# Banded attention layer of a two-layer mixer: both rows' scores ahead of the pair, a bias add behind the differences, two late checks in one place

## Chip, cores and metric

The kernel runs on one core of one Trainium2 chip. The metric is device time in microseconds of the one launch, as the median of three runs. All times below are microseconds unless marked ns. A core has TensorE (PE; its weight loads are listed apart as PEld), VectorE (DVE), ScalarE (ACT), GpSimd (POOL) and SyncE (SP, which issues most of the transfers). Each engine works through its own instructions in order and waits on semaphores of the others.

## What is computed

The input x is 128 rows of 256 positions of 256 channels, in float32. Two layers follow one another, each of the form x = x + layer(group norm of x). Layer 0 is a full attention with a bias from a second input z, a mask, and a gate. The change touches layer 1 alone: in each row an attention with 4 heads of 64 channels, in which position i sees only the positions within 16 of it.

```python
def _L1_conv_ref(x, w_in, b_in, w_out, b_out, band):   # band = 16, 4 heads
    qkv = x2 @ w_in.T + b_in
    q, k, v = jnp.split(qkv, 3, axis=-1)               # each cut into 4 heads of 64
    scores = jnp.einsum('bhid,bhjd->bhij', q, k) / jnp.sqrt(D)
    keep = jnp.abs(i - j) <= band
    attn = jax.nn.softmax(jnp.where(keep, scores, -jnp.inf), axis=-1)
    out = jnp.einsum('bhij,bhjd->bhid', attn, v)
    return out @ w_out.T + b_out
...
x = x + _L1_conv_ref(_gn(x), ...)
```

## The kernel before

**Tiling.** Layer 1 works through the 128 rows as 64 pairs of rows; row 0 and row 1 of a pair have 512 positions together. Channels lie on the partitions, in two chunks of 128 (`KC` = 2). The class `Pair1` holds one pair, and its methods each issue one step.

**The steps of a pair.** The constructor loads the pair twice through SP: `xs` in blocks to be transposed, and `xt` as it is, for the residual. `turn` (line 1860) transposes `xs` on DVE. `centre(k)` (line 1865) normalises one chunk on ACT into `xgT`; in the kernel before, the call for the second chunk also adds the output bias to `xt`, as one POOL instruction over 128x1024 elements (line 1870). `differences` (lines 1877 to 1880) makes four sums and differences of `xgT` on POOL, called t1 to t4, tile `dT`. They serve a scheme that forms the 2 by 2 block product of q, k and v by seven products instead of eight: `product(n, i)` issues product i for q (n = 0), k (n = 1) or v (n = 2) on PE (line 1915, for v line 1911) and, for four of the seven, an ACT instruction that takes the result out of PSUM (line 1924, for v 1922). `join(n, i)` (line 1931) adds a second PSUM tile to what ACT took out, on DVE. Products 6, 5, 7 and 4 read t2, t1, t3 and t4. Product 5 starts the second PSUM tile anew, so it waits for `join(n, 2)`, which reads that tile.

`scores(r)` (line 1968) makes the scores of row r on PE, 16 small products into two PSUM tiles; ACT takes the exponential (line 1977, two instructions) into an SBUF tile `e` with three buffers, and POOL multiplies by the band mask (line 1979, two instructions). `apply(r)` (line 1997) makes the weighted sums of v and the sums of the weights, the latter split over two halves of a PSUM tile. `copy_sums` (line 2012) and `copy_odd` (line 2015) bring them to SBUF on ACT. On DVE follow `join_sums` (line 2018, both inputs in SBUF), `join_odd` (line 2021), `invert` (line 2024, a reciprocal) and `weigh` (line 2029, both inputs in SBUF). `out_row` or `out_block` (line 2045) is the last projection on PE, `keep_row` (line 2053) adds the residual `xt` on DVE, and SP writes the result.

**PSUM.** Layer 1 uses eight PSUM tiles of 512 values a partition: four for what `apply` and the output projection write, and four handed out by `mm1(name, side)`, two buffers on side 0 and two on side 1. q's and v's products take side 0, k's take side 1, and both rows' scores take side 1.

**Order.** The order of the work is written out by hand: inside `tc.manual_schedule()` each engine gets its instructions in the order of the calls. A turn of the loop over p mixes three pairs: `was` (its row 1 is applied and put out), `now` (scores, and row 0 applied) and `nxt` (its products); `nn` is centred and differenced, and `n3` transposed. In the kernel before, `now.scores(0)` opens the turn and `now.scores(1)` stands in its middle, ahead of `now.apply(0)`. At the end of the turn come `nn.centre(1)`, `nn.differences()` and `n3.turn()`; the next turn's first DVE steps are `was.join_sums(1)` and `join(0, 2)`, and its first POOL steps the mask products.

**Checks.** The kernel checks some tiles against bounds on DVE, three instructions each (lines 958 to 960). `guard` checks the reciprocals of the last eight pairs, 128x512 at a time, in the middle of the turn. The others wait in the list `checks` and are taken one a turn: in turns 1 to 55 in the middle behind `guard`, in later ones at the end, behind `n3.turn()`. Four checks of the earlier pairs' sums, loaded in turn 58, fall into turns 58 to 61.

**Ahead of the loop**, pair 0 is centred and projected in full (`project`, line 1939; `values`, line 1954), then pair 1 is centred and differenced; then the mask and layer 0's sums are loaded through SP.

Of the kernel before, what the change touches and what calls it, by code (L numbers as in the profile page):

```python
# [9 lines left out]
F32 = mybir.dt.float32  # L10
# [11 lines left out]
def bcast(ap, axis, n):  # L22

    ap = ap.unsqueeze(axis)
    shape = list(ap.shape)
    shape[axis] = n
    return ap.broadcast_to(shape)
# [746 lines left out]
def fast_kernel(  # L774
# [1006 lines left out]
    with tc.tile_pool(name="l1", bufs=2) as sb, tc.tile_pool(  # L1781
# [5 lines left out]
        def mm1(name, side=0):  # L1787
            return ps_s.tile([P, 512], F32, name=name, tag=f"s{side}")
# [47 lines left out]
        class Pair1:  # L1836
# [25 lines left out]
            def centre(self, k):  # L1862
                if k == 0:
                    self.xgT = sb.tile([P, KC, N2], F32, name="xgT1", tag="xgT")
                nc.scalar.activation(
                    self.xgT[:, k, :], self.xT[:, k, :] if self.p else self.xT[k], AF.Identity,
                    bias=nM1[:, k : k + 1], scale=R1c[:, k : k + 1],
                )
                if k == KC - 1:
                    nc.gpsimd.tensor_tensor(self.xt, self.xt, bcast(bout_r, 1, 2 * NB), ALU.add)  # L1870

            def differences(self):

# [59 lines left out]
            def project(self, which, m):  # L1933
                n = ("qT", "kT").index(which)
                if m == 0:
                    setattr(self, which, sb.tile([P, KC, N2], F32, name=f"{which}1", tag=which))
                ps = mm1("ps_p1")
                for k in range(KC):
                    nc.tensor.matmul(
                        ps, w_in[:, k, n * C + m * P : n * C + (m + 1) * P], self.xgT[:, k, :],  # L1940
                        start=(k == 0), stop=(k == KC - 1),
                    )
                nc.scalar.activation(
                    getattr(self, which)[:, m, :], ps, AF.Identity, bias=bin_c[:, n * KC + m : n * KC + m + 1]
                )

            def values(self, r):
                if r == 0:
                    self.v = sb.tile([P, 2, NB, C], F32, name="v1", tag="v")
                ps = mm1("ps_v1")  # L1950
                for b in range(NB):
                    t = r * NB + b
                    for k in range(KC):
                        nc.tensor.matmul(
                            ps[:, b * C : (b + 1) * C], self.xgT[:, k, t * P : (t + 1) * P], w_in[:, k, 2 * C : 3 * C],
                            start=(k == 0), stop=(k == KC - 1),
                        )
                nc.scalar.copy(self.v[:, r, :, :].rearrange("p b c -> p (b c)"), ps)

            def scores(self, r):  # L1960

                ps = [mm1("ps_sc1", 1) for _ in range(2)]
                at = lambda q, c, j: ps[q][:, (c * 2 + j) * W : (c * 2 + j + 1) * W]
                for c in range(KC):
                    for k in range(NK):
                        for q in range(2):
                            rs = slice(q * D1, (q + 1) * D1)
                            nc.tensor.matmul(  # L1968
                                at(q, c, k // 2)[half(k)],
                                self.kT[rs, c, r * I + k * KB : r * I + (k + 1) * KB],  # L1970
                                self.qT[rs, c, r * I + q0(k) : r * I + q0(k) + W],
                                start=True, stop=True,
                            )
                e = sm.tile([P, 2, KC, NK // 2 * W], F32, name="e1", tag="e", bufs=3)
                ev = e.rearrange("p q c w -> p q (c w)")
                for q in range(2):
                    nc.scalar.activation(ev[:, q], ps[q][:, : KC * NK // 2 * W], AF.Exp)  # L1977
                for q in range(2):
                    nc.gpsimd.tensor_tensor(  # L1979
                        e[:, q], e[:, q], bcast(bw.rearrange("p b w -> p (b w)"), 1, KC), ALU.mult  # L1980
                    )
                self.es[r] = e
# [87 lines left out]
        def check_all(src, lo, hi):  # L2070
            for i in range(0, src.shape[1], 256):
                n = min(256, src.shape[1] - i)
                checks.append(lambda i=i, n=n: check(src[:, i : i + n], lo, hi, sm))

        def load_sums(src, name):
            t = sb.tile([P, src.shape[0] // P], F32, name=name, tag=name, bufs=1)
            nc.sync.dma_start(t, src.rearrange("(a b) -> a b", a=P))
            check_all(t, 1e-16, 1e8)

        with tc.manual_schedule():  # L2080
            now, nxt = pair1(0), pair1(1)
            now.turn()
            norm1()
            mix_weights()
            for k in range(KC):
                now.centre(k)
            nxt.turn()
            for m in range(KC):
                now.project("qT", m)
                now.project("kT", m)  # L2090
            for r in range(2):
                now.values(r)
            for k in range(KC):
                nxt.centre(k)
            nxt.differences()
        check_all(eb.rearrange("p h b i -> p (h b i)"), math.exp(-20.0), math.exp(20.0))
        mask_t = sb.tile([S, I], F32, name="mask_all", bufs=1)
        nc.sync.dma_start(mask_t, mask)
        check_all(mask_t, 1e-15, 1e15)
        load_sums(rsum.rearrange("n q r c i -> (n q r c i)"), "sums0")  # L2100

        with tc.manual_schedule():
            was = Nobody()
            for p in range(NP - 1):
                nn = pair1(p + 2) if p == 0 else n3
                n3 = pair1(p + 3)
                if p == 0:
                    nn.turn()
                if p == NP - LATE + 2:
                    load_sums(rsum1[: NP - LATE].rearrange("n q r i -> (n q r i)"), "sums1")  # L2110

                now.scores(0)
                was.apply(1)
                nxt.begin_fast()
                was.copy_sums(1)
                nxt.product(0, 1)
                was.copy_odd(1)
                nxt.product(1, 1)
                was.join_sums(1)
                for n in range(2):  # L2120
                    nxt.product(n, 2)
                    nxt.join(n, 2)
                was.invert(1)
                for i in (6, 5, 7):
                    for n in range(2):
                        nxt.product(n, i)
                for n in range(2):
                    nxt.join(n, 5)
                was.join_odd(1)
                was.weigh(1)  # L2130
                was.out_row(0)
                for n in range(2):
                    nxt.product(n, 4)
                    nxt.product(n, 3)
                    nxt.join(n, 3)
                fast = p < NP - 2
                if fast:
                    nxt.product(2, 1)
                    nxt.product(2, 2)
                    nxt.join(2, 2)  # L2140
                nn.centre(0)
                was.guard(1)
                if checks and 0 < p < NP - LATE:
                    checks.pop(0)()

                now.scores(1)
                now.apply(0)
                now.copy_sums(0)
                if fast:
                    nxt.product(2, 6)  # L2150
                    nxt.product(2, 5)
                now.copy_odd(0)
                now.join_sums(0)
                was.out_block(1, 0)
                if fast:
                    nxt.product(2, 7)
                now.join_odd(0)
                was.out_block(1, 1)
                if fast:
                    nxt.join(2, 5)  # L2160
                was.keep_row(1)
                if fast:
                    nxt.product(2, 4)
                    nxt.product(2, 3)
                    nxt.join(2, 3)
                now.invert(0)
                now.weigh(0)
                nn.centre(1)
                nn.differences()
                n3.turn()  # L2170
                if checks and p >= NP - LATE:
                    checks.pop(0)()
                was, now, nxt = now, nxt, nn
            assert not checks

# [8 lines left out]
            was.weigh(1)  # L2184
            was.out_row(0)
            now.scores(1)
            now.values(1)
            was.out_row(1)
            was.guard(1)
            now.apply(0)  # L2190
# [90 lines left out]
```

## Time and profile before

| what | us |
|---|---|
| median of 3 runs (lowest and highest) | 3168.44 (3167.47 to 3168.5) |
| the profiled execution's own time | 3168.98 |
| its span, first to last instruction | 3167.0 |
| mean granted TensorE clock | 0.984 |
| PE busy | 3030.7 (96%) |
| DVE busy | 2421.0 (76%) |
| POOL busy | 2292.6 (72%) |
| ACT busy | 1605.8 (51%) |

The profile is one execution. Its page lists busy time by engine, then the chain of work that ended last, then the costliest groups of instructions. Beside the page the trace answers finer questions: a timeline lists instructions by start, with their duration, their count where equal ones are merged, and in brackets the idle time of the engine ahead of them and what ended it; the waits sum up who waited for whom; a table of stretches gives each engine's busy time and the clock granted to PE. A DVE or POOL row's duration includes time in which the instruction has begun and does not get on. Layer 1 fills the time from about 1996 on, some 1165 of the 3167.

### The profile page before, as it was taken

The page shows a single profiled execution, that of the slowest core. Times are in us where ns is not written, and L with a number is a line of the kernel's source. Part 1 is how long each engine was busy: PE and PEld are TensorE (multiplying, and loading weights), DVE is VectorE, ACT ScalarE, POOL GpSimd, SP SyncE. Part 2 cuts the span into 40 slices and gives each one's busy share as a digit, 9 for nine tenths or more (in the row PEclk, how much of TensorE's full clock was granted, in tenths as well). Part 3 has the DMA queues.
Part 4 walks back from the last instruction along what each step waited for, and adds up shares of the span by engine and source line. Part 5 has one row for each costly group of instructions (what it writes and reads, how often), then busy time and mean ns, then how long its engine had stood idle before and what let it go on. Part 6 is the DMA issues. An engine that isn't in the chain of part 4 may idle for free.

```text
span 3167.0 us, 84747 instructions
## 1 busy us (share of the span) xinstructions
PE 3030.7 (96%) x35678; PEld 2112.9 (67%) x35678; DVE 2421.0 (76%) x3983; ACT 1605.8 (51%) x2637; POOL 2292.6 (72%) x1632
## 2 busy tenths in 40 slices
PE   5679999999999999999999999799999999999997
PEld 3345555556555555556555555688888888888886
DVE  7976677777777777777777777588888777777787
ACT  3454444444444444444444444455555555555553
POOL 3459899889888899988988896455555555555553
PEclk9789999999999999999999999899999999999999
DMA  9952333333333333343233432534343434343441
GB/s 360 391 169 52 98 69 97 98 80 82 94 91 70 98 97 95 71 98 92 66 96 92 98 72 65 123 86 98 82 103 82 100 86 97 88 94 91 93 98 36
DMA packets 690966, 328.42 MB, mean 104 GB/s; under 512 B 538672, under 2 KB 639920, under 8 KB 689424
## 3 DMA queue, kind: packets, MB, share of 16 engines
q1 hardware_dynamic: 686176, 320.28, 39.8%
q8 instruction: 282, 4.62, 0.6%
q10 hardware_dynamic: 4400, 2.63, 0.3%
q14 instruction: 108, 0.88, 0.1%
HBM read 254.09 MB, written 68.75 MB: 102 GB/s over the span
## 4 chain that ended last, share of the span: by engine, by line
PE 80%; DVE 9%; issue 5%; DMA 4%; POOL 2%; ACT 0%; SPq 0%; DVEq 0%; POOLq 0%; ACTq 0%
PE ps_p L1357 21%; PE ps_sc L1394 8%; PE ps_qk L1915 8%; PE ps_ov L1429 7%; PE ps_su_y L2045 7%; PE ps_y L1484 7%; PE ps_v L1375 7%; PE ps_qk L1911 7%; DVE rv L2024 3%; PE ps_su L1437 3%; PE ps_o L1997 2%; PE ps_sc L1968 2%; DVE xT L1860 2%; DMA xa<-in_x_dram 2%; DMA zt<-in_z_dram 1%
## 5 line engine op out<-in xcount | busy, mean ns | idle before, releaser
L1418 POOL TENSOR_TENSOR eboth<-e 128x512 f32<-128x512 f32 x512 | 745.6, 1477 | 175.9 <-PE ps_su L1437 95.9
L1414 DVE TENSOR_TENSOR e<-ps_sc,eb 128x1024 f32<-128x1024 f32 x384 | 458.3, 1221 | 288.6 <-ACT ps_sc L1406 288.5
L1979 POOL TENSOR_TENSOR e<-e,bw 128x384 f32<-128x384 f32 x256 | 262.0, 1045 | 487.8 <-ACT e L1977 487.8
L1406 ACT ACTIVATE ps_sc<-ps_sc 128x1024 f32<-128x1024 f32 x384 | 375.4, 1007 | 436.2 <-PE ps_sc L1394 309.7
L1394 PE MATMUL ps_sc<-qT,kT 32*128 32x256 f32 x4096 | 294.1, 400 | 0.8 <-DVE e L1414 0.8
L1394 PEld LDWEIGHTS ps_sc<-qT,kT 32*128 32x128 f32 x4096 | 185.3, 184 | 103.0 <-issue 90.7
L1484 PEld LDWEIGHTS ps_y<-wo,oT 128*128 128x128 f32 x1024 | 194.8, 191 | 84.2 <-issue 44.5
L2045 PE MATMUL ps_su_y<-w_out,oT 128*128 128x256 f32 x1008 | 249.3, 380 | 0.7 <-ACT sums L2012 0.7
L1357 PE MATMUL ps_p<-xnT,wq 128*128 128x512 f32 x512 | 247.6, 606 | 0.8 <-POOL xnT L1344 0.8
L1429 PE MATMUL ps_ov<-e,v 128*32 128x256 f32 x4096 | 248.0, 383 | 0.0
L1357 PE MATMUL ps_p<-xgT,wg 128*128 128x512 f32 x512 | 247.2, 605 | 0.1
L1484 PE MATMUL ps_y<-wo,oT 128*128 128x256 f32 x1024 | 243.5, 381 | 3.5 <-POOL oT L1474 2.7
L1375 PE MATMUL ps_v<-wv,xnT 128*128 128x256 f32 x1024 | 242.0, 379 | 1.6 <-ACT xgT L1326 1.6
L1357 PE MATMUL ps_p<-xnT,wk 128*128 128x512 f32 x512 | 240.6, 592 | 0.0
L1924 ACT ACTIVATE u<-ps_qk,bin_c 128x256 f32<-128x256 f32 x378 | 174.9, 477 | 115.9 <-PE ps_qk L1915 115.7
L1375 PEld LDWEIGHTS ps_v<-wv,xnT 128*128 128x128 f32 x1024 | 194.5, 190 | 55.9 <-issue 31.1
L2024 DVE RECIPROCAL rv<-sums 128x256 f32<-128x256 f32 x128 | 222.7, 1740 | 0.0
L1915 PE MATMUL ps_qk<-dT,wst 128*128 128x256 f32 x756 | 192.4, 391 | 19.0 <-DVE qT L1931 16.1
L2045 PEld LDWEIGHTS ps_su_y<-w_out,oT 128*128 128x128 f32 x1008 | 182.8, 191 | 21.0 <-ACT sums L2012 0.9
L1429 PEld LDWEIGHTS ps_ov<-e,v 128*32 128x32 f32 x4096 | 120.1, 110 | 109.0 <-issue 42.3
L2018 DVE TENSOR_TENSOR sums<-sums 128x256 f32<-128x256 f32 x128 | 104.8, 819 | 107.6 <-ACT sums L2012 107.6
L1915 PEld LDWEIGHTS ps_qk<-dT,wst 128*128 128x128 f32 x756 | 136.9, 191 | 63.8 <-DVE qT L1931 40.7
(229 smaller groups left out, 6470.9 us busy)
## 6 DMA issues: line engine op xcount, KB each, us to landing
xa<-in_x_dram SPq DMA_DIRECT2D x8, 4096.0 KB
xt<-in_x_dram SPq DMA_DIRECT2D x64, 512.0 KB
x<-xo SPq DMA_DIRECT2D x16, 2048.0 KB
xt<-x SPq DMA_DIRECT2D x64, 512.0 KB
rvb<-rsum SPq DMA_DIRECT2D x252, 128.0 KB
xs<-x SPq DMA_DIRECT2D x252, 128.0 KB
out_dram<-yo SPq DMA_DIRECT2D x63, 512.0 KB
xs<-in_x_dram SPq DMA_DIRECT2D x248, 128.0 KB
```

What stands on the lines that cost most here:

```text
L1357: nc.tensor.matmul(ps, w[:, k, m * P : (m + 1) * P], getattr(self, src)[:, k, :], start=(k == 0), stop=(k == KC - 1),)
L1375: nc.tensor.matmul(self.ps_v[:, b * C : (b + 1) * C], self.xnT[:, k, t * P : (t + 1) * P], wv[:, k, :], start=(k == 0), stop=(k == KC - 1),)
L1394: nc.tensor.matmul(self.pss[q // 2][:, q % 2, b, :], self.kT[rs, c, r * I + b * P : r * I + (b + 1) * P], self.qT[rs, c, r * I : (r + 1) * I],
L1406: nc.scalar.activation(self.pss[a], ps, AF.Exp)
L1414: nc.vector.tensor_tensor(es[a], pss[a], eb[:, h : h + 2], ALU.mult)
L1418: nc.gpsimd.tensor_tensor(t, es[a][:, :, 0, :], es[a][:, :, 1, :], ALU.add)
L1429: nc.tensor.matmul(ov[q * D0 : (q + 1) * D0, c, :], self.v[:, r, b, h * D0 : (h + 1) * D0], es[q // 2][:, q % 2, b, :], start=(b == 0), st ...
L1484: nc.tensor.matmul(self.ps_y[:, b * C : (b + 1) * C], self.oT[r][:, k, b * P : (b + 1) * P], wo[:, k, :], start=(k == 0), stop=(k == KC - 1),)
L1915: nc.tensor.matmul(to, lhs, rhs, start=start, stop=True, skip_group_check=True)
L1979: nc.gpsimd.tensor_tensor(e[:, q], e[:, q], bcast(bw.rearrange("p b w -> p (b w)"), 1, KC), ALU.mult)
L2024: nc.vector.reciprocal(self.rv[:, r, :], self.sums[:, 0])
L2045: nc.tensor.matmul(self.y[:, b], self.oT[r][:, k, b * P : (b + 1) * P], w_out[:, k, :], start=(k == 0), stop=(k == KC - 1),)
```

## The change

The diff does five things. `now.scores(1)` goes from the middle of the turn to directly behind `now.scores(0)`, and row r's scores take PSUM side 1 − r, so row 1's are on side 0. The bias add on POOL leaves `centre` and becomes `add_bias`, called for `nn` behind `nn.differences()`, and for pairs 0 and 1 behind pair 0's `values`. Pair 1 is centred in the loop of pair 0's projections, and its differences stand ahead of pair 0's `values`. All turns from 1 on take their check in the middle, behind `guard`. Mask and layer 0's sums are loaded at the start of turn 1, behind the loads of pair 4. `project` takes side m, and the last pair's `values(1)` takes side 1.

```diff
             def centre(self, k):
...
-                if k == KC - 1:
-                    nc.gpsimd.tensor_tensor(self.xt, self.xt, bcast(bout_r, 1, 2 * NB), ALU.add)
+
+            def add_bias(self):
+                nc.gpsimd.tensor_tensor(self.xt, self.xt, bcast(bout_r, 1, 2 * NB), ALU.add)
...
-                ps = mm1("ps_p1")
+                ps = mm1("ps_p1", m)
...
-            def values(self, r):
+            def values(self, r, side=0):
...
-                ps = mm1("ps_v1")
+                ps = mm1("ps_v1", side)
...
-                ps = [mm1("ps_sc1", 1) for _ in range(2)]
+                ps = [mm1("ps_sc1", 1 - r) for _ in range(2)]
...
             for m in range(KC):
                 now.project("qT", m)
                 now.project("kT", m)
+                nxt.centre(m)
+            nxt.differences()
             for r in range(2):
                 now.values(r)
-            for k in range(KC):
-                nxt.centre(k)
-            nxt.differences()
-        check_all(eb.rearrange("p h b i -> p (h b i)"), math.exp(-20.0), math.exp(20.0))
-        mask_t = sb.tile([S, I], F32, name="mask_all", bufs=1)
-        nc.sync.dma_start(mask_t, mask)
-        check_all(mask_t, 1e-15, 1e15)
-        load_sums(rsum.rearrange("n q r c i -> (n q r c i)"), "sums0")
-
-        with tc.manual_schedule():
+            now.add_bias()
+            nxt.add_bias()
+            check_all(eb.rearrange("p h b i -> p (h b i)"), math.exp(-20.0), math.exp(20.0))
+
             was = Nobody()
             for p in range(NP - 1):
...
+                if p == 1:
+                    mask_t = sb.tile([S, I], F32, name="mask_all", bufs=1)
+                    nc.sync.dma_start(mask_t, mask)
+                    check_all(mask_t, 1e-15, 1e15)
+                    load_sums(rsum.rearrange("n q r c i -> (n q r c i)"), "sums0")
...
                 now.scores(0)
+                now.scores(1)
                 was.apply(1)
...
                 was.guard(1)
-                if checks and 0 < p < NP - LATE:
+                if checks and p > 0:
                     checks.pop(0)()

-                now.scores(1)
                 now.apply(0)
...
                 nn.centre(1)
                 nn.differences()
+                nn.add_bias()
                 n3.turn()
-                if checks and p >= NP - LATE:
-                    checks.pop(0)()
                 was, now, nxt = now, nxt, nn
...
-            now.values(1)
+            now.values(1, 1)
```

## The prediction

> **What bounds the kernel now.** I read the page's chain of work first, then a timeline of one pair in the middle of layer 1, then the waits of PE.
>
> ```profile
> PE 80%; DVE 9%; issue 5%; DMA 4%; POOL 2%; ACT 0%; SPq 0%; DVEq 0%; POOLq 0%; ACTq 0%
> ```
>
> The chain is PE's, so a layer-1 pair costs what PE works plus what PE waits. In the timeline every pair has the same shape; this is the start of pair 14 (columns: start, duration, engine, line, operands, count, idle before it).
>
> ```profile
> 2259.80 0.89 PE L1968 MATMUL ps_sc<-qT,kT 64*64 64x96 f32 x32
> 2260.62 0.93 PE L1997 MATMUL ps_o<-e,v 64*32 64x96 f32 x60
> 2262.02 0.69 DVE L2029 TENSOR_TENSOR oT<-odd,rv 128x512 f32<-128x512 f32 x1
> 2262.07 1.24 POOL L1880 TENSOR_TENSOR dT<-xgT,dT 128x256 f32<-128x256 f32 x1
> 2262.63 1.24 DVE L1860 STREAM_TRANSPOSE xT<-xs 128x1024 f32<-128x1024 f32 x1
> 2263.27 2.14 POOL L1979 TENSOR_TENSOR e<-e,bw 128x384 f32<-128x384 f32 x2
> 2263.74 1.03 PE L1915 MATMUL ps_qk<-dT,wst 128*128 128x256 f32 x4
> 2263.79 0.76 DVE L2018 TENSOR_TENSOR sums<-sums 128x256 f32<-128x256 f32 x1
> 2264.47 0.41 DVE L1931 TENSOR_TENSOR qT<-ps_qk,u 128x256 f32<-128x256 f32 x1
> 2264.94 1.99 PE L1915 MATMUL ps_qk<-dT,wst 128*128 128x256 f32 x8 [0.17 <-DVE qT L1931]
> 2271.21 0.89 PE L1968 MATMUL ps_sc<-qT,kT 64*64 64x96 f32 x32
> 2272.03 0.93 PE L1997 MATMUL ps_o<-e,v 64*32 64x96 f32 x60
> 2277.50 0.89 PE L1968 MATMUL ps_sc<-qT,kT 64*64 64x96 f32 x32
> ```
>
> Call S the start of row 0's scores (2259.80). The next pair's S is 2277.50: one pair takes 17.70. Each scores block costs PE 0.82 (2259.80 to 2260.62; 2271.21 to 2272.03). PE has one wait: product 5 of q (the x8 row at 2264.94) overwrites a PSUM tile that DVE's join (2264.47) must have read. That join stands in DVE's queue behind reciprocal, weigh (2262.02), transpose (2262.63) and join_sums (2263.79). The four records before it start at 2263.74; at 0.213 apiece (eight take 1.70) product 5 could start at 2264.59. It starts at 2264.94 and, with its weight load uncovered, works as if from 2265.07 (the following group starts 1.83 later instead of 1.70). The stall is thus **0.48** a pair; PE's own work is 17.22.
>
> Now the point on which the forecast stands: why join_sums takes 0.76. It has two SBUF inputs, and POOL is at work. Rows of other places show what that does:
>
> ```profile
> 254.46 2.34 POOL L1282 TENSOR_TENSOR xt<-xt,bo_r 128x1024 f32<-128x1024 f32 x1
> 255.75 2.13 DVE L1414 TENSOR_TENSOR e<-e,eb 128x1024 f32<-128x1024 f32 x1
> ...
> 2326.84 1.00 POOL L1979 TENSOR_TENSOR e<-e,bw 128x384 f32<-128x384 f32 x1
> 2327.22 0.90 DVE L2018 TENSOR_TENSOR sums<-sums 128x256 f32<-128x256 f32 x1 [1.19 <-ACT sums L2012]
> 2327.80 2.54 POOL L1870 TENSOR_TENSOR xt<-xt,bout_r 128x1024 f32<-128x1024 f32 x1
> ```
>
> The mask multiply ends at 2327.84 and join_sums at 2328.12, 0.28 later, although it began 0.62 before that end. In layer 0 the bias add on POOL ends at 256.80 and DVE's product of two SBUF tiles, begun before, ends 1.08 later, at 257.88; begun with POOL idle such a product takes 1.22. So a two-SBUF DVE instruction that meets a running POOL instruction stands until that one ends. In reverse, dT's fourth difference takes 1.24 behind weigh, 0.73 elsewhere.
>
> The Trainium skill, "SBUF — State Buffer", section "Who interferes with whom", says the same against this change: a DVE instruction with two SBUF inputs contends with a GpSimd one that reads SBUF, and whoever issues first keeps the port for the whole instruction. If the port were shared by turns instead, the stall worked out below would go and the sum would be that of rival A.
>
> **Scores of row 1 beside row 0's, on PSUM side 0.** No instruction is added. PE's 0.82 moves from the middle (2271.21) to S+0.82. Apply of the old row 1 goes from S+0.82 to S+1.64, products 6 to 4.76 (before 3.94), and product 5 could start at 5.61. Side 0 is free in time: its last reader is DVE's join of v, S+0.11 to 0.53. ACT's second pair of exponentials (0.88) ends at 2.76 and product 1, which now takes side 0 after them, starts at 2.97; ACT's copy of the sums starts at 3.14, after apply, so they delay nothing. The three buffers of e suffice: the one taken was read a pair ago. If DVE stayed as it is, product 5 would find its tile at 5.27, before 5.61, and the 0.48 would be gone. What is late next is the bias add.
>
> **The bias add (line 1870) moves from before the four differences to behind them.** POOL's order becomes masks of both rows, differences, bias add. The differences wait as now for ACT's second centre (difference 2 at S+0.89), the fourth ends at S+3.51, and where the mask multiply stands now (2263.27) the bias add starts. It takes 2.34 when DVE leaves it alone (line 1870: least 2.345, median 2.542) and ends at S+5.81 (2265.61). join_sums cannot go ahead of it: DVE is free only at S+3.99. Its end becomes 2265.61 + 0.28 = 2265.89 instead of 2264.55, **1.34 later**, and the join and product 5 behind it likewise: product 5 at S+6.61 instead of 5.27. Both masks follow by S+9.9; row 0's is needed at S+12.7, so that costs nothing. In the middle POOL is now idle under join_sums (0.41 instead of 0.90), but DVE waits there anyway.
>
> After product 5 nothing else changes but the 0.82 that left the middle (the change of tile shape, 0.14, which a scores block pays after the v products, I let apply pay): 12.43 becomes 11.61. The pair takes 6.61 + 11.61 = 18.22, **+0.52**. Bounds: with the bias add at 2.54, +0.72; with the 0.14 not paid, +0.38; with no block at all, −0.48.
>
> **Late checks in one place.** Now a check of the sums, behind the transpose, costs a whole pair 1.79 (three pairs of 19.49) because it feeds the stall; after the last one PE also runs slowly:
>
> ```profile
> 3063.50:3083.00 19.50, 17.70 (x329) 15.23 (x329) 16.98 (x27) 10.41 (x22) 9.73 (x9) 1.00 0.36 82
> 3102.40:3106.00 3.60, 3.52 (x10) 2.85 (x11) 2.48 (x5) 0.95 (x2) 0.00 (x0) 0.64 0.00 0
> ```
>
> (Second column on: length, busy PE, PEld, DVE, ACT, POOL; then granted clock.) Beside the guard (0.41 + 0.69 + 0.69) the check (0.28 + 0.42 + 0.42 without POOL) makes the DVE work of the middle 1.1 longer than it is; the slack there is about 0.5 to the join before product 3 of v, and the first difference of dT can block the guard for up to 0.6. I take a stall of 0.8 (between 0 and 1.2) in pairs 58 to 61: 19.0 each. Now they take 17.70 + 3 × 19.49, and 1.9 for the slow stretch: 78.1 against 76.1, **−2.0**.
>
> The slow stretch came after PE had idled 1.96. The Trainium skill, "TensorE: Matmul & The Clock Gate", section "Part 1: The HAM clock gate", wants an idle window of some 3.4 us before the clock falls; the row shows a clock of 0.64 after less, so here the measurement decides. The new stall leaves PE idle about 1.0, and idling 1.53 in the pair at 3063.50 kept 1.00, so I add nothing.
>
> **Pair 1's input among pair 0's projections; mask and sums loaded later.**
>
> ```profile
> 2011.98 1.99 PE L1915 MATMUL ps_qk<-xgT,w_in 128*128 128x256 f32 x8 [1.67 <-ACT xgT L1865]
> 2016.73 4.33 PE L1915 MATMUL ps_qk<-dT,wst 128*128 128x256 f32 x12 [2.75 <-POOL dT L1878]
> 2024.72 0.93 PE L1997 MATMUL ps_o<-e,v 64*32 64x96 f32 x60
> ```
>
> PE waits 1.67 and 2.75 and runs slowly behind (12 records in 4.13 instead of 2.56). With centre under the projections (ACT idles 1.0 and more between them) and the differences done near 2010.6, PE makes both scores from 2009.42, starts products when the second exponential has left side 0 (near 2011.8), and works 1.83 + 2.56 + 1.73 + 0.99 with some 0.3 of waits: apply at 2019.2 instead of 2024.72, **−5.5** (bounds 0 and −7). The two bias adds and row 0's mask end near 2017.3, in time. Mask and sums loads (0.51 and 0.43 of SP's issue time) pass from ahead of pair 2's input to behind pair 4's, needed three pairs later: nothing; without that cover 0.94 once. The projections' own PSUM sides, and those of the last pair, free no wait that a row shows: nothing. Pair 62 has no v products: its lost scores block (1.2 there) against 0.47 more wait, −0.7.
>
> **Sum**, on the profiled execution (3168.98; span 3167.0 and 1.98 around it; the median of three is 0.54 lower): pairs 1 to 57, 57 × 0.52 = +29.6; late pairs −2.0; pair 62 −0.7; start −5.5. Together +21.4: **3190**.
>
> **Rivals.** A, faster: the block isn't met. It decides at the end of join_sums, 0.53 ahead of product 5: by S+5.1 there would be no stall, by S+5.6 no loss. For it speaks that today's stall is just this queue; against it the rows above, and 0.5 between the bias add's start (3.47) and join_sums (3.99). Pairs at 17.22: 57 × −0.48 = −27.4, late pairs −6.0, pair 62 −1.7, start −5.5: −40.6, **3128**.
> B, slower still: the bias add takes its median of 2.54 and the new neighbours cost 0.14 more at a change of shape: +0.34 × 62 = 21 on top, **3211**. For it: every add of the loop shows about 2.54; against: there DVE's sum was ahead of it in the port.
> C, the change cancels itself: the block lasts, but exponentials or the join of v come too late for side 0, or start and end give more; PE has about 1.0 of slack before product 5, so this hides: 3162 to 3175.
>
> **Numbers.** Forecast 0.68 (3175 to 3203), A and parts of it 0.17 (3125 to 3162), B 0.10 (3203 and more), C 0.05. A measurement here tells 0.2%, 6.3 us, from no change: faster 0.17, same 0.06, slower 0.77. The range 3165 to 3211 leaves out A and the top of B.
>
> **What would show it.** Right: the pair's period at 18.2; join_sums of row 1 lasting 2.1 and ending 0.28 behind the bias add; PE's wait for q's join near 1.0 in each pair; the middle join_sums at 0.41; apply of pair 0 near 10 us behind the first scores. Wrong: join_sums short with the bias add running over it, the bias add behind join_sums, or a period near 17.2.

## The result and the profile after

The changed kernel takes **3187.9** (median of 4 runs, 3187.05 to 3189.77) against 3167.95 (3166.9 to 3168.5) of the kernel before beside it: a ratio of 1.0064, interval 1.0047 to 1.0082. The prediction was 3190, slower. The profiled execution took 3188.32; its span is 3186.6, against 3167.0.

The chain that ended last, on the page of the kernel after, doesn't name the loss: DVE has less of it than before (4% against 9%), PE more.

```profile
PE 87%; issue 4%; DVE 4%; DMA 3%; POOL 2%; ACT 1%; ACTq 0%; SPq 0%; DVEq 0%; POOLq 0%
```

The same chain in order of time shows why, in the pair taken apart below (start, duration, engine or "issue", tile, line, count):

```profile
2318.74 1.94 PE ps_qk L1916 x8
2320.73 1.16 issue
2321.89 0.42 DVE qT L1932
2322.36 1.99 PE ps_qk L1916 x8
```

By the chain the join of q follows PE's work of 2320.7, but starts 1.16 later. Nothing that the chain knows releases it then, so the time is put down to "issue". What DVE did in it, the timeline of the kernel after tells, from row 0's scores on (S = 2315.86; columns: start, duration, engine, line, operands, count, idle before):

```profile
2315.86 1.55 PE L1969 MATMUL ps_sc<-qT,kT 64*64 64x96 f32 x64
2317.34 0.93 PE L1998 MATMUL ps_o<-e,v 64*32 64x96 f32 x60
2318.09 0.69 DVE L2030 TENSOR_TENSOR oT<-odd,rv 128x512 f32<-128x512 f32 x1
...
2319.33 2.35 POOL L1871 TENSOR_TENSOR xt<-xt,bout_r 128x1024 f32<-128x1024 f32 x1
2319.86 2.11 DVE L2019 TENSOR_TENSOR sums<-sums 128x256 f32<-128x256 f32 x1
2321.65 4.05 POOL L1980 TENSOR_TENSOR e<-e,bw 128x384 f32<-128x384 f32 x4
2321.89 0.41 DVE L1932 TENSOR_TENSOR qT<-ps_qk,u 128x256 f32<-128x256 f32 x1
2322.36 1.99 PE L1916 MATMUL ps_qk<-dT,wst 128*128 128x256 f32 x8 [0.69 <-DVE qT L1932]
```

The bias add ends at 2321.68, S+5.82. join_sums, begun 0.53 behind its start, is done at 2321.97, 0.29 behind its end: 2.11 for what took 0.76 before. Then come the join and product 5, for which PE stands idle. From another stretch of the same kernel: two applies of row 1 one pair apart, 18.24, and join_sums of row 0, which no POOL instruction meets in the middle (0.90 before).

```profile
2292.15 0.93 PE L1998 MATMUL ps_o<-e,v 64*32 64x96 f32 x60
...
2310.39 0.93 PE L1998 MATMUL ps_o<-e,v 64*32 64x96 f32 x60
...
2312.59 0.42 DVE L2019 TENSOR_TENSOR sums<-sums 128x256 f32<-128x256 f32 x1
```

The two largest waits of the weight loads in the kernel after from 2040 to 3050 (total, times, longest). The first line is the 1.1 a pair of product 5; not all of its records are in the trace. The second waits for nothing that the profile shows; the kernel before has no such line.

```profile
PEld ps_qk L1916 <- DVE qT L1932: 56.6, 51, 1.2
PEld ps_su_y L1998 <- issue: 8.7, 10, 1.7
```

**Where the time went**, counted from the start of one `join_odd` of row 0, in the middle of a turn, to the next (line 2021 before, 2022 after):

| stretch | before | after | difference | predicted |
|---|---|---|---|---|
| to the first middle | 2027.67 | 2021.62 | −6.05 | −5.5 |
| next 56 pairs | 990.99 | 1022.59 | +31.60 | +29.1 (56 × 0.52) |
| last 7 intervals and tail | 148.31 | 142.38 | −5.93 | −2.2 (0.5 − 2.0 − 0.7) |
| span | 3167.0 | 3186.6 | +19.6 | +21.4 |

### The profile page after: what moved, and what is told of

It is laid out like the page before. It is cut to its first block, busy times and chain, and to the rows that moved or that the text cites. A ratio compares the mean times of both kernels' runs of the same rounds, so it can differ in the third digit from the quotient of the medians.

```text
span 3186.6 us, 84747 instructions
## 1 busy us (share of the span) xinstructions
PE 3021.2 (95%) x35678; PEld 2111.3 (66%) x35678; DVE 2480.1 (78%) x3983; ACT 1600.8 (50%) x2637; POOL 2281.2 (72%) x1632
## 4 chain that ended last, share of the span: by engine, by line
PE 87%; issue 4%; DVE 4%; DMA 3%; POOL 2%; ACT 1%; ACTq 0%; SPq 0%; DVEq 0%; POOLq 0%
PE ps_p L1357 21%; PE ps_qk L1916 11%; PE ps_sc L1394 8%; PE ps_ov L1429 7%; PE ps_su_y L2046 7%; PE ps_y L1484 7%; PE ps_v L1375 7%; PE ps_qk L1912 6%; PE ps_o L1998 3%; PE ps_su L1437 3%; PE ps_sc L1969 3%; PE ps_su_y L1998 2%; DMA xa<-in_x_dram 2%; DMA zt<-in_z_dram 1%; DVE st L1192 1%
## 5 line engine op out<-in xcount | busy, mean ns | idle before, releaser
L1879 POOL TENSOR_TENSOR dT<-xgT,dT 128x256 f32<-128x256 f32 x63 | 46.1, 731 | 300.1 <-ACT xgT L1865 300.1
L1878 POOL TENSOR_TENSOR dT<-xgT 128x256 f32<-128x256 f32 x63 | 45.9, 729 | 236.9 <-ACT xgT L1865 236.9
L2019 DVE TENSOR_TENSOR sums<-sums 128x256 f32<-128x256 f32 x128 | 151.8, 1186 | 53.3 <-ACT sums L2013 53.2
```

## The experiments

The theory T (theory P in the expectations): the loss is join_sums of row 1, a DVE instruction with two SBUF inputs, standing until the whole bias add on POOL ends. Its rivals: Q, the loss comes from the scores' new place and PSUM side; R, the join of q is late for its place in DVE's queue however short join_sums is. The ratios are to the kernel before, run beside each kernel on the same chip; a pair is the median of the 56 intervals counted above.

| kernel | median (runs) | ratio, interval | pair (median) | join_sums row 1 |
|---|---|---|---|---|
| after | 3187.9 (4) | 1.0064, 1.0047 to 1.0082 | 18.23 | 2.11 |
| bias add before the differences | 3151.4 (4) | 0.9948, 0.9931 to 0.9965 | 17.49 | 0.75 |
| late bias add alone | 3260.43 (4) | 1.0293, 1.0276 to 1.031 | 19.05 | 2.10 |
| scores side by side alone | 3160.92 (10) | 0.9979, 0.9969 to 0.9989 | 17.49 | 0.75 |
| late checks alone | 3165.28 (11) | 0.999, 0.9981 to 0.9999 | 17.70 | 0.75 |
| new start alone | 3164.38 (11) | 0.9985, 0.9976 to 0.9994 | 17.70 | 0.75 |
| bias add in four | 3141.43 (4) | 0.9918, 0.9901 to 0.9935 | 17.17 | 0.48 |
| sum from PSUM | 3140.27 (4) | 0.9914, 0.9899 to 0.9929 | 17.31 | 0.38 |
| four adds in POOL's gap | 3141.29 (4) | 0.991, 0.9893 to 0.9926 | 17.17 | 0.75 |
| gap and PSUM | 3141.73 (4) | 0.9916, 0.99 to 0.9933 | 17.17 | 0.38 |
| scores apart, PSUM | 3137.17 (4) | 0.9905, 0.9889 to 0.9922 | 17.33 | 0.38 |
| before, PSUM | 3145.69 (4) | 0.9932, 0.9916 to 0.9949 | 17.33 | 0.39 |

**One line back: the bias add before the differences.**

```diff
 (kernel after)
-                nn.differences()
-                nn.add_bias()
+                nn.add_bias()
+                nn.differences()
```

> The changed kernel with one step put back: in the loop POOL makes the bias add ahead of the four differences again, right behind the four mask products. Theory P (a two-input DVE instruction stands until the running POOL instruction ends): join_sums of row 1 now meets a mask product of 1.0 and ends near S+4.75 instead of S+6.1, so product 5 no longer waits; but the bias add now runs from about S+7.5 to S+9.9, and weigh of row 1, due at about S+8.9, has two SBUF inputs too: it is held up by some 0.9, and through the join behind it product 2 of v waits about 0.5. A pair of about 17.6 instead of 18.24, in all about 3148 (if weigh is not held up, 17.1 and 3117). Rival Q (the cost is the scores' new place: the second pair of exponentials ahead of the sums, and products waiting for side 0): nothing changes, 3188.

In this kernel's timeline join_sums is short and weigh is the one that stands: the bias add ends at 2315.57, weigh 0.55 later. (0.69 is weigh's length with POOL idle.)

```profile
2309.73 0.75 DVE L2019 TENSOR_TENSOR sums<-sums 128x256 f32<-128x256 f32 x1
...
2313.21 2.36 POOL L1871 TENSOR_TENSOR xt<-xt,bout_r 128x1024 f32<-128x1024 f32 x1
...
2314.67 1.45 DVE L2030 TENSOR_TENSOR oT<-odd,rv 128x512 f32<-128x512 f32 x1
...
2317.11 0.52 PEld L1912 LDWEIGHTS ps_qk<-w_in,xgT 128*128 128x128 f32 x4 [0.34 <-DVE qT L1932]
```

The order of two POOL instructions is worth 36.5 of 3187.9. Everything else of the change is in this kernel, and it is faster than before: Q falls. The hold has not gone; it has moved to weigh, which has more slack: PE waits some 0.3 behind it.

**The late bias add alone.**

```diff
 (kernel before; centre no longer adds the bias)
+            def add_bias(self):
+                nc.gpsimd.tensor_tensor(self.xt, self.xt, bcast(bout_r, 1, 2 * NB), ALU.add)
...
                 nn.differences()
+                nn.add_bias()
```

> The kernel before with one step of the change: in the loop the bias add comes behind the differences; the scores stay where they were. Theory P: join_sums ends near S+6.1 as in the changed kernel, and with row 1's scores still in the middle the whole 1.34 is lost: a pair of 19.04 instead of 17.70, in all about 3248. Rival Q: the scores are untouched, so 3168, no change.

A pair and its parts, in this kernel's timeline: the same 2.10 for join_sums, and 1.90 of idle time ahead of product 5's weights.

```profile
2299.45 2.35 POOL L1871 TENSOR_TENSOR xt<-xt,bout_r 128x1024 f32<-128x1024 f32 x1
...
2299.99 2.10 DVE L2019 TENSOR_TENSOR sums<-sums 128x256 f32<-128x256 f32 x1
...
2302.48 1.59 PEld L1916 LDWEIGHTS ps_qk<-dT,wst 128*128 128x128 f32 x8 [1.90 <-DVE qT L1932]
```

A pair takes 19.05, 1.35 more than before: the delay of join_sums in full, since PE has no second scores block to put in front of product 5. The period agrees with T to 0.01; the total is above 19.04 a pair because the late checks stand in the same queue (pairs of 21.2 to 22.9). This edit costs 92 alone and 36.5 beside the rest of the change.

**The scores side by side alone.**

```diff
 (kernel before)
-                ps = [mm1("ps_sc1", 1) for _ in range(2)]
+                ps = [mm1("ps_sc1", 1 - r) for _ in range(2)]
...
                 now.scores(0)
+                now.scores(1)
...
-                now.scores(1)
                 now.apply(0)
```

> The kernel before with the scores of row 1 behind row 0's, on PSUM side 0, and nothing else (the bias add stays ahead of the differences). Theory P: as with the bias add put back in the changed kernel, a pair of about 17.6, so 57 times -0.1: 3162, and the late checks and the start as before; without the hold of weigh 17.1 and 3133. Rival Q: this alone makes the loss, a pair of 18.2, 3198.

A pair takes 17.49, 0.21 less than before. Side 0 and the new place cost nothing that the period shows; with the old place of the bias add the median of weigh is 1.375, held as in the first experiment.

**The late checks alone, and the start alone.**

```diff
 (kernel before, first experiment)
-                if checks and 0 < p < NP - LATE:
+                if checks and p > 0:
...
-                if checks and p >= NP - LATE:
-                    checks.pop(0)()
 (kernel before, second experiment)
             for m in range(KC):
...
+                nxt.centre(m)
+            nxt.differences()
...
-            for k in range(KC):
-                nxt.centre(k)
-            nxt.differences()
+            now.add_bias()
+            nxt.add_bias()
```

> The kernel before with the checks of the last turns in the middle of the turn, and nothing else. If the 1.79 that each costs at the end of the turn comes from standing ahead of join_sums, and if the middle has room for it: three pairs of 19.49 and the slow stretch behind them come down to about 17.7 to 18.5, -4 to -7, 3162 to 3164. If the middle only moves the wait (product 3 of v stalls by 1.1 instead): -2 or less, 3166 to 3168.

> The kernel before with pair 1 centred among pair 0's projections, its differences ahead of pair 0's values, and the two bias adds of these pairs behind; the loop is that of the kernel before. The first apply comes about 6 earlier, and if nothing takes it back later the total falls by as much: 3162. If a transfer or a later wait takes it back: 3168.

In the second kernel the bias add of the loop stays ahead of the differences, and `project` takes side m. Checks: the total is 3.2 lower, between the two forecasts; the last 8 intervals take 143.38 against 145.87, −2.5. A pair with a check still takes 19.0 to 20.2, so by the periods the middle mostly moves the wait from one place to another in the old order. Start: the first middle comes at 2021.15 instead of 2027.67, −6.5, and the loop keeps its 17.70; but the total falls by 4.1 only (3164.38 against 3168.45). In the profile 1.6 is lost again behind the 56 pairs, where pairs with a check take 21.17, 19.49 and 21.17 against 19.48, 19.49 and 21.18 before. The later loads of mask and sums were not run alone.

**The bias add in four.**

```diff
 (kernel after)
-                nc.gpsimd.tensor_tensor(self.xt, self.xt, bcast(bout_r, 1, 2 * NB), ALU.add)
+                for t in range(2 * NB):
+                    nc.gpsimd.tensor_tensor(self.xt[:, t, :], self.xt[:, t, :], bout_r, ALU.add)
```

> The changed kernel with the bias add as four POOL instructions over 128x256 instead of one over 128x1024, in the same place. Theory P with a hold that lasts for one instruction: join_sums at S+4.0 meets one quarter (about 0.7) and ends near S+4.6, product 5 no longer waits; the masks end about 0.5 later, so weigh may meet one mask product. A pair of 17.1 to 17.3, in all 3118 to 3132. If the hold lasted for all of POOL's queued work, or if the order of the scores were the cause (rival Q): 3188 or a little more.

The same work on POOL in the same place, in four pieces (3.03 together instead of 2.35), and join_sums is free within its own length. This is the timeline of that kernel:

```profile
2324.36 3.03 POOL L1872 TENSOR_TENSOR xt<-xt,bout_r 128x256 f32<-128x256 f32 x4
2325.00 0.43 DVE L2020 TENSOR_TENSOR sums<-sums 128x256 f32<-128x256 f32 x1
2326.01 2.75 PE L1917 MATMUL ps_qk<-dT,wst 128*128 128x256 f32 x12
```

POOL's work has grown and yet 46 has gone: it isn't POOL's load that costs, but the length of the one instruction that DVE meets. PE no longer waits before product 5 (twelve records without a gap), and a pair takes 17.17. The total is 9 above the expected range. The 56 intervals last 16.4 more than 56 × 17.17; what that is stands at the end.

**One SBUF input fewer.** The copy of row 1's sums is cut in half, and join_sums reads the other half in PSUM.

```diff
 (kernel after)
-                nc.scalar.copy(self.sums, su_y[:, :, 0])
+                if r == 1:
+                    nc.scalar.copy(self.sums[:, 1], su_y[:, 1, 0])
+                else:
+                    nc.scalar.copy(self.sums, su_y[:, :, 0])
...
-                nc.vector.tensor_tensor(self.sums[:, 0], self.sums[:, 0], self.sums[:, 1], ALU.add)
+                first = su_y[:, 0, 0] if r == 1 else self.sums[:, 0]
+                nc.vector.tensor_tensor(self.sums[:, 0], first, self.sums[:, 1], ALU.add)
```

> The changed kernel with row 1's join_sums reading one half of the sums straight from PSUM: ACT copies only the other half (128x256), so DVE's instruction has one SBUF input instead of two. POOL's order is untouched. Theory P: join_sums lasts 0.42 at S+4.0 while the bias add runs on, product 5 no longer waits, the bias add still ends at S+5.8; weigh of row 1 (due S+8.9) may meet the last mask product. A pair of 17.1 to 17.5, in all 3118 to 3145. Rival R (product 5 is late because DVE's queue of reciprocal, weigh, transpose is long, and the port is beside the point): the join comes no earlier than the shorter copy allows, a gain of 0.1 a pair at most, 3180 or more.

This kernel's timeline has the bias add whole and join_sums in the middle of it:

```profile
2304.52 2.36 POOL L1871 TENSOR_TENSOR xt<-xt,bout_r 128x1024 f32<-128x1024 f32 x1
...
2305.05 0.38 DVE L2023 TENSOR_TENSOR sums<-ps_su_y,sums 128x256 f32<-128x256 f32 x1
...
2305.71 2.75 PE L1916 MATMUL ps_qk<-dT,wst 128*128 128x256 f32 x12
```

The queue of DVE, its order and POOL's work are those of after, and join_sums begins 0.53 behind the bias add's start as it did there, so ACT's shorter copy doesn't matter; the second SBUF input is gone, and with it the 2.11. Weigh of row 1 stands at 1.20 in the median (0.69 in after); whether that makes 17.31 of 17.17 is not shown. R falls, and T holds from both of its sides, the POOL instruction's length and the DVE instruction's inputs.

**The add in POOL's gap, without and with PSUM.** POOL idles 4.8 between the first and the second difference in the kernel after.

```diff
 (kernel with the bias add in four; differences calls it behind its first instruction)
-                nn.differences()
-                nn.add_bias()
+                nn.differences(nn.add_bias)
```

> The kernel after with the loop's bias add as four adds of 128x256, placed on POOL between the first and the second difference, where POOL stood idle for 4.8 us of a pair. Theory (what costs is the DVE instruction with two SBUF inputs standing behind whole POOL instructions at join_sums of row 1): join_sums of row 1 now meets at most a mask product and lasts 0.42 to 0.5; weigh of row 1 lasts 0.69 to 0.85; a pair 17.05 to 17.15, as in the kernel with the add in four, or 0.1 less; the pauses of PE that wait for nothing shown stay (about 10 in all); total 3125 to 3142, about 3137. Rival (POOL's work in the middle of the pair now holds join_sums or the joins of the middle, or delays the second difference and with it product v): a pair of 17.4 and more, total 3150 and more, with join_sums of row 0 at 0.8 or more.

> The kernel with the four adds between the differences, and join_sums of row 1 reading one half of its sums from PSUM, so that it has one SBUF input. Theory: join_sums of row 1 waits for nothing any more in the kernel it is made from, so there is nothing left to win: 0 to 3 us less than that kernel, join_sums of row 1 at 0.38. Rival (join_sums still holds up product 5, or ACT's shorter copy brings weigh and the next pair forward): over 5 us less.

The two kernels take 3141.29 and 3141.73, with a pair of 17.17 in both. In the first, join_sums of row 1 takes 0.75, not the 0.42 to 0.5 expected: what runs on POOL then is a mask product. The second adds the edit of the sum from PSUM (0.38). But nothing waits for the 0.75: from 2290 to 2870 of the first kernel's trace the weight loads wait for q's join once, 0.4. From here on PE's own work is the bound, with the pauses described at the end, and this other place for POOL's work gives nothing.

**Scores apart again, without the hold; and the kernel before without it.**

```diff
 (first: kernel with the sum from PSUM)
-                ps = [mm1("ps_sc1", 1 - r) for _ in range(2)]
+                ps = [mm1("ps_sc1", 1) for _ in range(2)]
...
                 now.scores(0)
-                now.scores(1)
...
+                now.scores(1)
                 now.apply(0)
 (second: kernel before)
+                if r == 1:
+                    nc.scalar.copy(self.sums[:, 1], su_y[:, 1, 0])
...
-                nc.vector.tensor_tensor(self.sums[:, 0], self.sums[:, 0], self.sums[:, 1], ALU.add)
+                first = su_y[:, 0, 0] if r == 1 else self.sums[:, 0]
+                nc.vector.tensor_tensor(self.sums[:, 0], first, self.sums[:, 1], ALU.add)
```

> The kernel after with row 1's scores back in the middle of the turn, on PSUM side 1, and with join_sums of row 1 reading one half of its sums from PSUM; the later bias add, the checks in one place and the new start stay. It tells what the two scores blocks side by side are worth once join_sums is not held, and whether PE's pauses that wait for nothing shown come from the three blocks of small products in a row. Theory: join_sums of row 1 lasts 0.38 instead of the 0.75 of before, so that PE's wait of 0.48 for q's join falls to 0.1 to 0.2; a pair takes 17.3 to 17.4; no pauses in apply of row 1 (0 instead of about 10), so every pair is within 0.3 of the median; total 3130 to 3142. Rival (the pauses come from elsewhere, such as the place of the instructions in the program): about 10 pauses stay, and the total is 3145 or more.

> The kernel before with nothing changed but join_sums of row 1 reading one half of its sums from PSUM, and ACT copying only the other half. Theory (the kernel before lost its 0.48 a pair to join_sums standing behind POOL's mask product): join_sums of row 1 0.38 instead of 0.75, a pair 17.3 to 17.4 instead of 17.70, total 3144 to 3152. Rival (the join of q is late for its place in DVE's queue, whatever join_sums takes): a pair stays at 17.6 to 17.7, total 3160 to 3168.

Both pairs take 17.33. In the kernel before, changing what join_sums reads wins 22: 0.37 of its 0.48 a pair was the same hold, at the mask product. The rest of the change, with the scores apart, wins 8.5 more; in the profile it lies in the start (−5.7) and behind the 56 pairs (−7.5), and these pairs give 3.1 back. The kernel with the scores apart has the lowest median here, 3137.17. These are the waits of its weight loads from 2040 to 3050; the line of pauses is gone:

```profile
PEld ps_qk L1916 <- DVE qT L1932: 12.1, 57, 0.8
PEld ps_qk L1912 <- issue: 0.3, 1, 0.3
```

## Why the prediction was right, point by point

- **join_sums stands until the POOL instruction ends.** Right, to 0.01 in the kernel after: 0.29 behind the end, predicted 0.28. Shown by the experiments from both sides. Held instructions of three lengths end 0.14 less than their free length behind POOL's: join_sums 0.28 (free 0.42), weigh 0.55 (free 0.69), layer 0's product 1.08 (free 1.22). By these rows a held instruction does nearly all of its work after the hold, and how far into the POOL instruction it began earns it nothing. The Trainium skill, "SBUF — State Buffer", section "Who interferes with whom", calls the port pair that DVE shares with GpSimd an exclusive lock, and says that a DVE instruction with two SBUF inputs contends with a GpSimd instruction that reads SBUF. The 2.11 of after and, with one input in PSUM, the 0.38 of the sum from PSUM agree with it.
- **The bias add starts at S+3.47, takes 2.34, and join_sums cannot be ahead of it.** Right: S+3.47, 2.35, and join_sums starts 0.53 behind (predicted 0.52).
- **Product 5 at S+6.61, a pair of 18.22.** Right: its records start at S+6.50 with the weight load uncovered, and the period is 18.23. The 56 pairs cost 2.5 more than 56 × 0.52. Of that 0.6 is the 0.01 of the period, and 1.9 is mostly three pairs of 18.9, which are among those in which PE pauses. Both masks end at S+9.84 (predicted 9.9), and nothing waits for them.
- **Row 1's scores cost PE 0.82 wherever they stand.** Slightly off: both blocks take 1.48 together, not 1.64. In the loop this is hidden under the wait; where the hold is gone a pair takes 17.17, against the 17.22 of rival A.
- **The start, −5.5.** Measured −6.05 in after and −6.5 alone. The first scores begin at 2008.82 and apply follows 9.84 later (predicted near 10), at 2018.66, in the timeline of after:

```profile
2008.82 1.63 PE L1969 MATMUL ps_sc<-qT,kT 64*64 64x96 f32 x64
...
2011.06 1.99 PE L1916 MATMUL ps_qk<-xgT,w_in 128*128 128x256 f32 x8 [0.62 <-ACT e L1978]
...
2018.66 0.93 PE L1998 MATMUL ps_o<-e,v 64*32 64x96 f32 x60
```

- **Late pairs at 19.0 each: mis-sized.** They take 19.48, 18.18, 18.2 and 17.84, 73.7 instead of 76.0 (77.85 before); and the pair behind them, with what follows, is 2.4 shorter rather than 0.7. The step that failed is the stall of 0.8 in the middle. This is a late pair of after, timeline and the answer for its stretch (length, busy PE, PEld, DVE, ACT, POOL; then granted clock, DMA share, GB/s):

```profile
3083.11 0.71 PE L1912 MATMUL ps_qk<-wst,xgT 128*128 128x128 f32 x4 [0.29 <-DVE v L1932]
...
3085.46 0.73 POOL L1881 TENSOR_TENSOR dT<-xgT,dT 128x256 f32<-128x256 f32 x1
3086.15 2.81 POOL L1871 TENSOR_TENSOR xt<-xt,bout_r 128x1024 f32<-128x1024 f32 x1
...
3087.83 1.42 DVE L2019 TENSOR_TENSOR sums<-sums 128x256 f32<-128x256 f32 x1
...
3089.64 1.99 PE L1916 MATMUL ps_qk<-dT,wst 128*128 128x256 f32 x8 [0.22 <-DVE qT L1932]
```

```profile
3090.00:3108.00 18.00, 17.50 (x329) 15.16 (x328) 16.58 (x26) 10.19 (x22) 9.44 (x10) 1.00 0.46 91
```

  PE does wait in the middle, but DVE, being late, meets POOL elsewhere: the last difference is not held (0.73, not 1.24), the bias add starts sooner, join_sums meets only its last 1.1, and the wait at product 5 falls from 0.69 to 0.22. One wait replaced another; I had added them. The clock stayed at 1.00, behind the last check too (3136 to 3144), so the slow stretch of before (1.9) is gone as counted; and the stall of each pair, with PE idle 0.69 and its weight loads 1.1, did not lower it either (mean 0.985, before 0.984).
- **Rivals.** A did not happen; its price was nearly right for a pair (17.17 against 17.22), but the kernels that take the block away stand at 3140 to 3142, not 3128: the three blocks side by side bring pauses that I did not know of. B: its 2.54 falls; the bias add of after has a median of 2.35. C: the gains at start and end were there, 12.0 instead of 7.7, and too small.
- **The sum, 3190 for 3187.9.** The pair is right by its mechanism. That the total is closer than its parts is luck: the 56 pairs cost 2.5 more than forecast, in good part by pauses that I did not know of, and the start and the end gave 4.3 more.

## What to carry to other kernels

Before moving a long GpSimd instruction, look which VectorE instruction with two SBUF inputs will start while it runs, and how much slack that one has: it pays what is left of the GpSimd instruction. The cure need not be the order: cut the GpSimd instruction in pieces (−46), or let VectorE read one input from PSUM (−48). A place on an idle engine is not free until what it holds up there has been looked at, and two waits in one queue are not added before asking whether the first takes the place of the second.

## What was not expected of the hardware

**PE pauses when three blocks of small products stand together.** In all seven kernels with scores, scores and apply in a row PE stops inside apply's last products for up to 1.7, waiting for nothing that the profile shows, 10 to 15 times between 2040 and 3050; the other six, the kernel before among them, have no such wait. This is the kernel with the bias add in four:

```profile
2531.39 0.58 PE L1999 MATMUL ps_su_y<-e,ones 64*32 64x96 f32 x29
2533.37 0.10 PEld L1999 LDWEIGHTS ps_su_y<-e,ones 64*32 64x32 f32 x1 [1.62 <-issue]
```

With one of the two scores blocks taken out of the burst, the pauses are gone: the kernel with the scores apart has no such wait, and its 56 intervals exceed 56 × 17.33 by 3.3, of which 2.8 is the first. It differs from the kernel with the sum from PSUM in the place of row 1's scores and their PSUM side alone, so these are shown as the condition. Between these two the order wins nothing: a pair takes 17.31 with the scores together and 17.33 with them apart, the excess over the median is 8.1 against 3.3, and the times, 3140.27 and 3137.17, don't tell the two orders apart for sure (their intervals overlap). The pairs of 17.17 also have the bias add in four pieces, and the scores apart were not run with that.

What PE waits for is argued, not shown. The long pairs are mostly the same ones in these kernels, and come again seven pairs later (in gap and PSUM, counted from 0: intervals 8, 15, 22, 29, 36, 43, 50, and a shorter series two behind). The page counts a queue of instruction transfers, here of the bias add in four (packets, MB, share):

```profile
q8 instruction: 282, 4.62, 0.6%
```

That is 16 KB a packet; in the loop one starts each 6.8 or so, 18 in seven pairs of 17.4. The pause above ends 1.5 after such a packet had landed (started 2530.2, took 1.7), and those of 2655.3 and 2777.8 end 1.3 and 1.5 after theirs. So do the others: all 13 of this trace end 1.2 to 1.6 behind a landing, all 10 of the kernel after 1.0 to 1.6. A packet alone is not enough: 149 start between 2040 and 3050 here, and 150 in the kernel with the scores apart, which never pauses. PE waiting for its instructions would explain the repeat; no experiment here changed the fetch itself.

**Other holds.** With the scores together, weigh of row 1 stands at a median of 1.37 behind a bias add in its old place (0.69 with POOL idle), and in the kernel after a check's second instruction takes 1.00 instead of 0.42 beside the first difference; the transpose (1.24) and joins with an input from PSUM (0.41) keep their lengths beside POOL's instructions.
